# x1 = x + G p3: from two VectorE additions per pair to ScalarE copies and one accumulating DMA

## The chip, the cores and the metric

The kernel runs on 1 core of one Trainium2 chip. The metric is the device time of one execution in microseconds; three runs of the kernel before gave 2427.26, 2429.36 and 2429.52, so the median is 2429.36 us.

## The reference

Two layers work on x, 64 matrices of 256 x 256 in float32, with one adjacency matrix `adj` of 256 x 256.

```python
# --- layer 0 (adj_preln) ---
h = jnp.maximum(_layernorm(x, axis=-1), 0.0)
x = x + _L0_gnn_ref(h, adj, adj, L0_gnn_W1, L0_gnn_W2, L0_gnn_W3)
# --- layer 1 (adj_preln) ---
h = jnp.maximum(_layernorm(x, axis=-1), 0.0)
x = x + _L1_gnn_ref(h, adj, L1_gnn_W1, L1_gnn_b1, L1_gnn_W2, L1_gnn_b2)
```

Layer 0 multiplies three times by G = adj * adj and by a weight, with relu between: relu(G h W1), relu(G . W2), G . W3. Layer 1 needs U, the eigenvectors of the normalized Laplacian of adj (`jnp.linalg.eigh`), and computes U (relu(U^T h W1 + b1) W2 + b2). The sum that the change touches is the one that ends layer 0: x1 = x + G p3, with p3 = relu(...) W3.

## The kernel before

Two kinds of work share the core up to some 2250 us. The first is the eigenvector computation, class `Eigen`, called the chain here: tridiagonalization in 254 steps (`tridiagonalize`), then leaves, then four levels of merging. It is one long dependence, mostly small VectorE operations; a step also has two transposes on PE (`psB<-ident,ac` and `psA<-ident,A`, of a column that VectorE has just finished, `ac`), a square and a root on ScalarE and small operations on POOL (`m`, `q`, `qn`, `qs`, `gg`, `gu`, `none`, `xc`; in the second half of the steps only some of them).

The second is layer 0, class `Layers`, which doesn't need U. It runs over 32 pairs of matrices. It comes as two streams, that is, generators that yield one operation at a time:

- `products` yields for pair q: `third` (32 products of 512 columns, in the profile `bank<-y,L_gnn_W`), `turn_rows(q - 1)` (transposes, `bank<-eye,h`), half of `fourth` (256 columns, `bank<-L_gnn_W,s`), `for_layer1(q - 1)`, `first(q + 1)`, the other half of `fourth`, `second(q + 1)` and `last(q)` (four products of 512 columns, `bank<-p,gt`). Each group of products ends in a PSUM bank, of which there are four, and ScalarE empties it.
- `rows` yields the layer norms on ScalarE, with small VectorE operations between: `begin(q)` of x, and `norm1(q - 1)` of x1, whose result `turn_rows` transposes.

`last(q)` is the place of the change. Before, VectorE reads each of its two banks and adds x to it (`x<-x,bank`). Then SP writes x1 to DRAM ("spill"; not for the last two pairs), and `third(q + 1)` follows in the same generator.

The class `Pace` writes the order of all of this out by hand. It holds an estimated clock for each engine and, from the costs in `Op`, the time at which each tile is written or free (`busy` is how long an operation holds its engine, `until` when its result is there). For each operation of the chain, `chain` computes when it is due, and `run` first records operations of the streams that can start before that; of each stream only the operation at its head is seen (`Stream.head`). An operation that can't start before the limit stays at the head, and what is behind it in the generator stays unseen. PE and ScalarE keep the order that is so recorded (`manual_schedule`); VectorE, POOL and SP are ordered by the framework's scheduler. What is left of the streams when the chain has ended runs between the rounds of `layer1`, whose operations are all kept in the recorded order, and `pace.finish()` records the rest when round i = 8 begins (`LAST_AT - 1 - ahead`).

In the profile nearly all instructions have line 209, the line in `issue` that calls the recorded operation, or 213. They are told apart by their tiles.

Of the kernel before, what the change touches and what calls it, by code (L numbers as in the profile page):

```python
# [23 lines left out]
OP = mybir.AluOpType  # L24
# [58 lines left out]
class Op:  # L83
# [4 lines left out]
    def __init__(self, part, call, args, kwargs):  # L88
        self.part, self.engine, self.call, self.args, self.kwargs = part, ENGINES[part], call, args, kwargs
        self.name = call.__name__  # L90
        free = lambda a: int(np.prod([int(n) for n in a.shape[1:]]))
        named = dict(kwargs)
        outs = [named.pop("out")] if "out" in named else [args[0]]
        ins = [a for a in [*(args if "out" in kwargs else args[1:]), *named.values()] if isinstance(a, bass.AP)]
        total = named.pop("accum_out", None)
        if isinstance(total, bass.AP):
            outs.append(total)
            ins = [a for a in ins if a is not total]
        self.outs, self.ins = [span(a) for a in outs], [span(a) for a in ins]
        n = max(free(a) for a in outs[:1] + ins) if self.engine == "DVE" else free(outs[0])  # L100
        sums = len(outs) > 1

        if self.engine == "PE":
            self.columns = 0 if "transpose" in self.name else n
            self.busy = max(n * self.COLUMN, 0.224) if self.columns else 0.115
            self.until = max(self.busy, 0.165) + 0.35
        elif self.engine == "ACT":
            pointers = any(isinstance(kwargs.get(k), bass.AP) for k in ("scale", "bias"))
            self.busy = 0.13 + n / 1400 + 0.12 * pointers + 0.19 * sums
            self.until = self.busy + 0.12  # L110
        elif self.engine == "DVE":
            each = 6.3 if self.name == "reciprocal" else 2.0 if self.name == "tensor_tensor_scan" else 1.0
            pointers = self.name == "scalar_tensor_tensor" or any(a.shape[1:] == [1] for a in ins[1:])
            self.busy = 0.065 + 0.06 * pointers + each * n / 960 + 0.08 * sums
            self.until = self.busy + 0.125
        elif self.engine == "POOL":
            self.busy = 0.2 + 2 * n / 960
            self.until = self.busy + 0.1
        else:
            self.busy, self.until = 0.1, 4.0  # L120
# [13 lines left out]
def span(a):  # L134

    step = a.ap[0][0]
    lo = a.offset % step if step else a.offset
    return a.tensor.name, lo, lo + sum((int(n) - 1) * abs(int(s)) for s, n in a.ap[1:]) + 1
# [142 lines left out]
class Eigen:  # L281
# [998 lines left out]
    def level(self, n, qt, dc, rho, sg, bad=None):  # L1280
# [93 lines left out]
        def spread(ps, column):  # L1374

            for h in range(H):
                nc.tensor.matmul(
                    ps if last else ps[:, seg[h]],
                    lhsT=column[:, h : h + 1].to_broadcast([P, P]),
                    rhs=perm[:, h, :],  # L1380
                    start=h == 0 or not last,
                    stop=h == H - 1 or not last,
                )
# [349 lines left out]
class Layers:  # L1733
# [138 lines left out]
    def rows(self):  # L1872

        for q in range(PAIRS + 1):
            if q < PAIRS:
                if q > 0:
                    yield lambda: q - 1 in self.begun
                yield from self.begin(q)
            if q > 0:
                yield lambda: q - 1 in self.new  # L1880
                yield from self.norm1(q - 1)
# [101 lines left out]
    def last(self, q):  # L1983

        nc, x, p3 = self.nc, self.x.pop(q), self.p3.pop(q)
        x1 = self.kept.tile([P, H, 2, N], F32, tag="x1", name="x1")
        for m in range(H):
            ps = self.bank()
            yield from self.products_of(ps, [(self.gt2[:, h, m * P : (m + 1) * P], p3[:, h, :]) for h in range(H)])
            yield nc.vector.tensor_tensor(flat(x1)[:, m, :], flat(x)[:, m, :], ps, OP.add)  # L1990
        if q in self.spilled:
            yield nc.sync.dma_start(out=self.spilled[q], in_=x1.rearrange("p h b f -> p (h b f)"))
        else:
            self.x1[q] = x1
        self.new[q] = x1
# [111 lines left out]
    def layer1(self, pace):  # L2107


        ahead = 3  # L2110
        last = PAIRS - 1
        order = [*range(LAST_AT - 1), last - 1, last, *range(LAST_AT - 1, last - 1)]
        got = {i: self.fetch(order[i]) for i in range(ahead)}
        mid, tail = {}, {}
        with self.tc.manual_schedule():
            self.turn()
            pace.go_on(LOAD_US)
            for i in range(PAIRS + 2):
                if i == LAST_AT - 1 - ahead:
                    self.due = True  # L2120
                    pace.finish()
                if i + ahead < PAIRS:
                    got[i + ahead] = self.fetch(order[i + ahead])
                if i < PAIRS:
                    mid[i] = self.to_vectors(*got.pop(i))
                if 0 <= i - 1 < PAIRS:
                    s, xb = mid.pop(i - 1)
                    tail[i - 1] = self.from_vectors(s), xb
                if 0 <= i - 2:
                    self.finish(order[i - 2], *tail.pop(i - 2))  # L2130


def flat(t):
    return t.rearrange("p h b f -> p h (b f)")
# [63 lines left out]
```

## Time and profile before

| | us |
|---|---|
| median of three runs | 2429.36 |
| the profiled execution: first to last instruction | 2426.6 |
| PE idle in waits over 0.3 us, summed from the trace | 37.9 |
| tridiagonalization, from the first `ac` to the last | 21.9 to 1322 |
| VectorE's additions `x<-x,bank`, first and last start | 105.3 to 2249.8 |

The profiled execution's own time is its span; it lies 0.1% under the median and within 0.7 us of the fastest run. A row of the profile gives an engine, an operation, the written tile, an arrow and the read tiles, then how often, the busy time and the mean of one. In an order of time the first two columns are start and duration in us, and the brackets at the end give how long the engine stood idle before and what ended that. A float32 product appears as two records of PE, so that `x8` is four products. How full PE is over the span, in 40 equal slices, with the granted clock and the DMA engines below:

```profile
PE   7999999999999999999999899999999999999999
...
DVE  8999999999999999999999989999997888886443
ACT  4444454444444444344444244344344434443322
POOL 2334333343333111111111000000000000000443
PEclk9999999999999999999999999999999999999999
DMA  3000000000000000000000000000000000000676
```

DMAs before the change, with size and median time from issue to landing; all are issued by SP:

```profile
x<-x SPq DMA_DIRECT2D x60, 512.0 KB, 3.6
x<-in_x_dram SPq DMA_DIRECT2D x64, 256.0 KB, 3.7
```

The first row holds the spills of x1 and their loads back in layer 1.

### The profile page before, as it was taken

Reading aid. Unit: us, or ns where it says so; the run is one execution under the profiler, and the core shown is the slowest. Engines: PE = TensorE matmul, PEld = TensorE weight load, DVE = VectorE, ACT = ScalarE, POOL = GpSimd, SP = SyncE. Lnnn points to the kernel's source line nnn. Section 1 sums busy time; section 2 is a strip of 40 time slices with the busy share of each in tenths; the row PEclk is TensorE's granted clock in tenths of the full one; section 3 lists DMA queues with packets and bytes.
Section 4 is the critical chain, followed back from the end, with each engine's and each line's share of the span. In section 5 each row is a group of like instructions: output and inputs, shape, how many; then the busy total and the mean of one; then the engine's idle time right before and its main releaser. Section 6 shows DMA issues by size and latency. Waiting matters only on the chain. (4 is left out here: it accounts for less than half of the span.)

```text
span 2426.6 us, 38393 instructions
## 1 busy us (share of the span) xinstructions
PE 2381.5 (98%) x9226; PEld 1581.7 (65%) x9226; DVE 2127.2 (88%) x12971; ACT 1013.8 (42%) x2827; POOL 480.6 (20%) x1752
## 2 busy tenths in 40 slices
PE   7999999999999999999999899999999999999999
PEld 4666666666666566666666666666566666666788
DVE  8999999999999999999999989999997888886443
ACT  4444454444444444344444244344344434443322
POOL 2334333343333111111111000000000000000443
PEclk9999999999999999999999999999999999999999
DMA  3000000000000000000000000000000000000676
GB/s 113 18 21 7 23 23 18 23 23 23 6 23 23 18 22 23 22 6 23 23 23 26 10 23 23 23 23 22 18 22 27 22 23 12 16 22 1 210 255 204
DMA packets 59399, 90.02 MB, mean 37 GB/s; under 512 B 5792, under 2 KB 42784, under 8 KB 59168
## 3 DMA queue, kind: packets, MB, share of 16 engines
q1 hardware_dynamic: 59168, 87.52, 10.8%
q8 instruction: 74, 1.21, 0.2%
q14 instruction: 157, 1.29, 0.2%
HBM read 47.13 MB, written 40.37 MB: 36 GB/s over the span
## 5 line engine op out<-in xcount | busy, mean ns | idle before, releaser
L209 PE MATMUL bank<-y,L_gnn_W 128*128 128x512 f32 (+2 forms) x2182 | 903.5, 566 | 1.1 <-ACT y L209 1.1
L209 PEld LDWEIGHTS bank<-y,L_gnn_W 128*128 128x128 f32 x2182 | 401.8, 190 | 440.7 <-issue 419.0
L209 PE MATMUL bank<-L_gnn_W,s 128*128 128x256 f32 (+1 forms) x2092 | 465.2, 375 | 3.2 <-ACT s L209 3.2
L209 PEld LDWEIGHTS bank<-L_gnn_W,s 128*128 128x128 f32 x2092 | 386.7, 190 | 52.2 <-ACT s L209 3.9
L209 ACT ACTIVATE s<-bank 128x512 f32<-128x512 f32 x384 | 224.9, 586 | 196.4 <-PE bank L209 196.0
L209 PE MATMUL bank<-gt,s 128*128 128x256 f32 x1036 | 233.7, 379 | 2.8 <-ACT s L209 2.8
L209 PE MATMUL bank<-L_gnn_W,y 128*128 128x512 f32 (+2 forms) x542 | 230.9, 569 | 1.1 <-ACT y L209 1.1
L209 PEld LDWEIGHTS bank<-gt,s 128*128 128x128 f32 x1036 | 194.7, 191 | 39.7 <-issue 10.5
L209 ACT COPY y<-bank 128x512 f32<-128x512 f32 x192 | 111.5, 582 | 138.9 <-PE bank L209 138.6
L209 PEld LDWEIGHTS bank<-L_gnn_W,y 128*128 128x128 f32 x542 | 100.2, 190 | 97.3 <-issue 91.1
L209 POOL COPY m<-xr 128x1 f32<-128x1 f32 x254 | 55.8, 220 | 534.5 <-DVE xr L209 526.5
L209 ACT ACTIVATE s<-nn,guard 128x1 f32<-128x1 f32 x254 | 74.5, 293 | 208.1 <-DVE nn L209 169.0
L209 ACT ACTIVATE h<-x,shift,scale 128x256 f32<-128x256 f32 x256 | 137.3, 589 | 54.6 <-DVE shift L209 54.4
L209 ACT ACTIVATE junk<-x 128x256 f32<-128x256 f32 x256 | 105.6, 412 | 95.8 <-DVE x L209 80.5
L209 ACT ACTIVATE junk<-x,nm 128x256 f32<-128x256 f32 x256 | 129.0, 504 | 37.1 <-DVE nm L209 32.6
L209 DVE SCALAR_TENSOR_TENSOR A<-xr,wc,A 128x255 f32<-128x255 f32 (+63 forms) x381 | 139.9, 368 | 0.0
L209 DVE SCALAR_TENSOR_TENSOR A<-wr,q,A 128x255 f32<-128x255 f32 (+63 forms) x381 | 138.9, 366 | 0.0
L209 ACT ACTIVATE junk<-xr 128x254 f32<-128x254 f32 (+63 forms) x127 | 46.0, 362 | 216.5 <-DVE xr L209 211.4
L209 DVE SCALAR_TENSOR_TENSOR q<-q 128x1 f32<-128x1 f32 (+1 forms) x576 | 119.8, 208 | 13.0 <-ACT q L209 2.3
L209 PE MATMUL bank<-gt,h 128*128 128x256 f32 (+1 forms) x518 | 120.6, 382 | 0.1
L209 POOL TENSOR_TENSOR xb<-x,ub 128x512 f32<-128x512 f32 x16 | 19.9, 1271 | 495.5 <-DMA hw<-hw 485.6
L209 PE MATMUL bank<-p,gt 128*128 128x512 f32 (+2 forms) x270 | 117.0, 570 | 0.1
(615 smaller groups left out, 4306.2 us busy)
## 6 DMA issues: line engine op xcount, KB each, us to landing
x<-x SPq DMA_DIRECT2D x60, 512.0 KB, 3.6
x<-in_x_dram SPq DMA_DIRECT2D x64, 256.0 KB, 3.7
out_dram<-out SPq DMA_DIRECT2D x64, 256.0 KB, 2.2
hw<-hw SPq DMA_DIRECT2D x60, 256.0 KB, 2.7
L_gnn_W<-in_L_gnn_W_dram SPq DMA_DIRECT2D x1, 2048.0 KB, 10.9
L_gnn_W<-in_L_gnn_W_dram SPq DMA_DIRECT2D x1, 1024.0 KB, 13.5
L_gnn_W<-in_L_gnn_W_dram SPq DMA_DIRECT2D x1, 512.0 KB, 6.3
mask<-in_c_blk_dram SPq DMA_DIRECT2D x2, 256.0 KB, 3.1
```

What stands on the lines that cost most here:

```text
L209: return op.call(*op.args, **op.kwargs)
```

## The change

ScalarE now copies each of the two banks of `last` into x1, and one DMA per pair, issued by GpSimd (POOL), adds x to x1 in place; 64 additions on VectorE become 64 copies on ScalarE and 32 DMAs of 512 KB. The planner's costs get a line for such a DMA: it holds POOL for 1.1 us, and its result is there 5.0 us after its start.

```diff
@@ Op.__init__
             self.busy = 0.065 + 0.06 * pointers + each * n / 960 + 0.08 * sums
             self.until = self.busy + 0.125
+        elif self.engine == "POOL" and "dma" in self.name:
+            self.busy, self.until = 1.1, 5.0
         elif self.engine == "POOL":
             self.busy = 0.2 + 2 * n / 960
             self.until = self.busy + 0.1
@@ Layers.last
         for m in range(H):
             ps = self.bank()
             yield from self.products_of(ps, [(self.gt2[:, h, m * P : (m + 1) * P], p3[:, h, :]) for h in range(H)])
-            yield nc.vector.tensor_tensor(flat(x1)[:, m, :], flat(x)[:, m, :], ps, OP.add)
+            yield nc.scalar.copy(flat(x1)[:, m, :], ps)
+        rows = lambda t: t.rearrange("p h b f -> p (h b f)")
+        yield nc.gpsimd.dma_start(out=rows(x1), in_=rows(x), accum_op=OP.add)
         if q in self.spilled:
             yield nc.sync.dma_start(out=self.spilled[q], in_=x1.rearrange("p h b f -> p (h b f)"))
         else:
```

## The prediction

> **What bounds the kernel now.** I read the busy shares first, then the matrix engine's waits.
>
> ```profile
> PE 2381.5 (98%) x9226; PEld 1581.7 (65%) x9226; DVE 2127.2 (88%) x12971; ACT 1013.8 (42%) x2827; POOL 480.6 (20%) x1752
> ...
> L209 DVE TENSOR_TENSOR x<-x,bank x64: 624/680/689, 105.3 to 2249.8; 128x512 f32<-128x512 f32 x64
> ...
> PE bank L209 <- ACT s L209: 6.5, 7, 2.4
> PE psC L209 <- DVE c L209: 6.3, 1, 6.3
> ...
> PE psB L209 <- DVE xr L209: 3.9, 8, 1.0
> ...
> PE psB L209 <- DVE ac L209: 3.2, 6, 1.1
> ```
>
> PE is busy for 2381.5 of 2426.6 us, and its waits of over 0.3 us sum to 38. The end is therefore set by how full the planner keeps PE's queue: the time that an engine beside it saves is worth nothing in itself, and every hole in the order of PE's products is lost. Where holes can come from shows in PE's order of time around one `last` (four 512-wide products are eight records here).
>
> ```profile
> 946.23 0.27 PE L209 MATMUL psB<-ident,ac 128*128 128x128 f32 x1
> ...
> 950.56 0.27 PE L209 MATMUL psB<-ident,ac 128*128 128x128 f32 x1
> ...
> 951.21 3.60 PE L209 MATMUL bank<-p,gt 128*128 128x512 f32 x8
> 955.44 0.29 PE L209 MATMUL psB<-ident,ac 128*128 128x128 f32 x1 [0.62 <-DVE xr L209]
> 955.57 0.27 PE L209 MATMUL psA<-ident,A 128*128 128x128 f32 x1
> 955.68 1.88 PE L209 MATMUL bank<-y,L_gnn_W 128*128 128x512 f32 x4
> ```
>
> Between two pairs of the chain's transposes (`psB<-ident,ac`) lies one step of the tridiagonalization, filled with products of layer 0. After `last` (`p,gt`) the next pair's `third` (`y,L_gnn_W`) follows at once. The chain has hardly a margin: its own part of a step shows on VectorE.
>
> ```profile
> 953.70 0.68 DVE L209 TENSOR_TENSOR x<-x,bank 128x512 f32<-128x512 f32 x1
> ...
> 955.07 0.22 DVE L209 SCALAR_TENSOR_TENSOR ac<-A,m,xa 128x1 f32<-128x1 f32 x1
> ```
>
> From the transpose at 950.56 the chain needs until 955.29 to have the next `ac`, plus 0.15 to PE's start: 4.88 us, of which the add is 0.68, so 4.20 without it. Products for less than that in a step leave PE idle.
>
> **The change part by part.**
>
> *The adds go.* 64 x 0.68 = 43.4 us leave VectorE. They bind PE only where PE waited for a step with an add: waits such as the 0.62 above, 5.6 us over the tridiagonalization. This is the only direct gain.
>
> *Copies come.* 64 copies of 128x512 at 582 ns (row `y<-bank`, 111.5 us for 192) are 37 us on ScalarE, 42% busy. They empty a bank in 0.58 us in place of 0.68, and four banks cover some 14 us of products: nothing. Were ScalarE full, it would be 37.
>
> *The hole behind every DMA (the main term).* `products` is one generator, and the planner sees one operation of it at a time. Behind `last`'s copies it now gives the DMA, then the spill on SP, then the products of the next `third`. The planner's new branch has the DMA's result ready 5.0 us after its start, so the spill can't start sooner, and `run` records it only when the chain's next due time lies beyond. Until then the chain's transposes go into PE's queue with no products between them. Before, an add stood there, 0.72 us in the planner's costs (0.065 + 512/960 + 0.125). The built program's order shows it: 18 of the first 253 steps hold under 3.1 us of products (at 14 of the 18 pairs; six hold only the two transposes), where neighbours hold 3.5 to 6. A 512-wide product costs 0.86 us: five between 1104.05 and 1108.34 in PE's order of time. A 256-wide costs 0.43: seven between 1086.16 and 1089.18. So priced, the 18 steps hold 23.9 us in all. The chain's part of these steps, worked out as above at each and taken as the median of nine neighbours, is 6.2 us at the first and 3.5 to 3.7 at the last, 81.3 in sum. PE idles 81.3 - 23.9 = 57.4. From the other side: when the tridiagonalization ends (1322 us now), the new order has 76.7 us less of products behind it. The chain can be shorter by its 36 adds at most, 24.5; so the loss is at least 52.2, and 76.7 if it gets no shorter. Four pairs have no such step, but fall short by less; I let that stand against the 5.6 gained and take **57**, ends 52 and 76.7. After the tridiagonalization the deficit grows by only 15 us up to the flag, as much as the adds of 12 pairs (16): no further loss there.
>
> *The clock behind a hole.* The granted clock fell twice in this execution.
>
> ```profile
> 1344.74 1.19 PE L209 MATMUL psD<-bs,mask 128*128 128x128 f32 x4 [2.77 <-DVE rb L209]
> ...
> 1343.00:1346.00 3.00, 1.26 (x5) 1.29 (x6) 3.00 (x26) 0.69 (x2) 0.00 (x0) 0.74 0.00 0
> 1346.00:1350.00 4.00, 3.56 (x16) 2.84 (x15) 2.60 (x18) 0.96 (x2) 0.00 (x0) 0.77 0.17 66
> ...
> 1715.56 4.97 PE L209 MATMUL bank<-gt,s 128*128 128x256 f32 x14 [2.40 <-ACT s L209]
> ```
>
> The column behind POOL's is the granted clock: 3 x 0.26 + 4 x 0.23 = 1.7 us lost behind a gap of 2.77, and after the gap of 2.40 seven products took 4.81 in place of 3.02. A gap of 1.57 at 2251 cost nothing (clock 1.00). The new holes are 2.3 to 5.1 us long at 14 places; I charge 13 of them 1.7: **22**, ends 0 (the fall lies wholly in the gap) and 44. [...]
>
> *The end of layer 0 (second term).* `layer1` ends the streams at its eighth round. Before, pair 31's `last` ended at 2249.75 and its `turn_rows` began at 2289.10, with layer 1's products between. The new order, 92 us of products behind at the flag, has `turn_rows` of pair 31 directly behind its `last`. PE then waits for copy, DMA and norm. The norm lasts from 2199.09 to 2206.68 at pair 30 with two evictions in it, 6.5 without. The DMA isn't in this trace. Below stands the spill of the same 512 KB, 3.6 us to landing; above the load of 2048 KB, 10.9. I take 5.5, near the spill: a second operand is another 512 KB, 1.6 us at the 334 GB/s of q1 (87.52 MB in 10.8% of 2426.6), and 0.3 for the issue. 0.8 + 5.5 + 6.5 less 1.2 that the first transposes gain: **12**, ends 10 and 17, and 1.7 for the clock. [...]
>
> *What queues behind.* On POOL the DMA's issue stands between the chain's small operations; POOL waits 1.07 to 3.0 us for VectorE before `gg` and `m`, and 17 of the 18 DMAs of this stage stand ahead of such a wait. An issue costs between SP's 0.34 and 1.27 (POOL's longest operation, `xb`). On ScalarE `norm1`'s first reading waits for the landing, and the chain's square and root behind it. It was placed for 5.0 us; a landing d later costs about d x d / (2 x 5.1) for each of 18 pairs (step 5.1 us, next chain operation at a random place): nothing at 5.5, 61 us at 10.9. The chain has no margin, so I take **4** for both, ends 0 and 84. On SP the next x load waits behind the spill for some 5 us more; its norm ends 7 us or more before its first product in every pair now, and `norm1` 9.9 before `turn_rows`: covered, and some 2 us a pair for seven pairs if the DMA took 10.
>
> Sum: 57 + 22 + 13.7 + 4 = 97. The profiled execution, 2426.6 of span, is taken to stand for the median, 2429.4 (0.1% away). **2526 us.**
>
> **Rivals.** (1) *A slow DMA*: it lands after 8 to 11 us and ScalarE's queue carries the wait into the chain. For: two operands, and an issue from an engine that is 30% busy in this stage (391.66 of 1305 us). Against: the same bytes land in 3.6. At 10.9: 61 + 5 more, 2592. (2) *Short holes only*: the clock costs nothing and the holes 52, the end 10: 2491; a little under it if some holes are filled. For: the fall of the clock comes some 2.4 us after the gap's start and lasts 3.4, so part of it lies inside the longer holes. (3) *Not slower*: VectorE's chain, not PE, sets the end; rid of 43.4 us it ends sooner and pulls the rest along, 2386. For: VectorE is 88% busy and the chain has no margin. Against: PE idles for only 38 us in all. It decides only if the products missing in the holes run elsewhere in time that was idle, which is less than the 57 needed. (4) *Nothing*: the holes are of the plan alone and don't show. The trace has PE's instructions in the program's order throughout, so I see no way.
>
> **How the numbers follow.** The forecast (2491 to 2555) has 0.72, the slow DMA 0.14, under 2491 but slower 0.10, (3) 0.02, (4) 0.02. The range 2485 to 2575 leaves out half of the slow DMA and most of the smaller loss. A change within 0.2% (5 us) can't be told from none here. Faster 0.02, same 0.02, slower 0.96.
>
> **What would show it.** Right: PE waits for `psB<-ident,ac` of 2.3 to 5 us once per pair up to about 1310 us, new and some 60 us in sum; a granted clock of 0.7 to 0.8 behind them; one wait of about 12 us before the last `eye,h`; PE's busy time up by the clock alone. Wrong: `junk<-x` on ScalarE waiting for a DMA by more than 1 us in most pairs (rival 1), POOL's `qs` or `gg` late, or PE's waits as short as now.

## The result, and the profile after

The changed kernel takes 2524.16 us (median of 4 runs, 2523.11 to 2524.55); the kernel before, run beside it, 2429.44 (4 runs). The ratio is 1.0392, 95% interval 1.0378 to 1.0405: 95 us slower. The profiled execution has a span of 2521.3 us, against 2426.6.

The page of the changed kernel: busy shares, PE over the span, POOL's issues of the new DMAs, and the DMA's median time to landing.

```profile
PE 2409.3 (96%) x9198; PEld 1589.8 (63%) x9198; DVE 2088.6 (83%) x12907; ACT 1049.9 (42%) x2891; POOL 509.5 (20%) x1784
...
PE   7999999999999999999999999999999999999799
...
L211 POOL DMA_DIRECT2D x<-x x32 | 28.6, 895 | 546.9 <-ACT x L211 463.1
...
x<-x POOLq DMA_DIRECT2D x32, 512.0 KB, 4.6
```

VectorE lost 38.5 us of work (2127.2 to 2088.6), ScalarE gained 36.1, and neither shows in the time. PE decides: it is busy 27.8 us longer (2409.3 against 2381.5) though it computes the same products, and it is idle for 112.0 us (2521.3 - 2409.3) where it was idle for 45.1. 27.8 + 66.9 is the whole difference of the spans, 94.7. So there are two things to find: the idle time, and why the same products take longer.

The idle time, from PE's waits in the changed kernel (total us, times, longest):

```profile
PE psB L211 <- DVE xr L211: 57.5, 29, 5.0
PE bank L211 <- ACT h L211: 15.6, 5, 12.6
...
PE psB L211 <- DVE ac L211: 4.6, 1, 4.6
```

The first row was 3.9 us in 8 before. The second has one wait of 12.6 us at the end of layer 0. One of the waits for `xr`, behind the first `last`, in order of time (start, duration; the brackets hold the idle time before and what ended it):

```profile
105.10 0.38 PE L211 MATMUL psB<-ident,ac 128*128 128x128 f32 x2
...
105.54 0.81 PE L211 MATMUL bank<-p,gt 128*128 128x384 f32 x2
...
107.29 1.07 POOL L211 DMA_DIRECT2D x<-x  x1 [1.74 <-ACT x L211]
...
111.38 0.40 PE L211 MATMUL psB<-ident,ac 128*128 128x128 f32 x2 [5.03 <-DVE xr L211]
...
111.97 1.06 PE L211 MATMUL bank<-y,L_gnn_W 128*128 128x512 f32 x1
112.03 0.34 SPq L211 DMA_DIRECT2D x<-x  x1
```

The step from 105.10 to 111.38 holds 0.81 us of products. The next pair's `third` (`y,L_gnn_W`) comes only behind the next transpose, at 111.97. None of its products reads what the DMA writes; they simply stand behind it in PE's order. The engine that "released" PE, VectorE, was on its ordinary chain.

The same products take longer because of the clock. In the windows of the changed kernel around that hole (PE busy is the second number, the granted clock stands before the last two):

```profile
109.00:112.00 3.00, 0.62 (x5) 0.65 (x6) 2.73 (x17) 0.05 (x1) 1.62 (x7) 0.95 0.86 162
112.00:115.00 3.00, 3.00 (x5) 1.30 (x5) 2.95 (x13) 1.26 (x6) 0.78 (x3) 0.50 0.70 226
115.00:118.00 3.00, 3.00 (x8) 1.31 (x7) 2.90 (x16) 2.13 (x9) 1.61 (x6) 0.98 0.35 123
```

PE is "busy" throughout 112 to 115, but at half clock (0.50). The records of 512 columns start every 0.85 us from 111.97 to 114.53 and every 0.43 us from 115.25 on: in 3.4 us behind the hole PE gets done what takes 1.7 at the later pace.

### The profile page after: what moved, and what is told of

It reads as the page before. It is cut to its first block, busy times and chain, and to the rows that moved or that the text cites. A ratio compares the mean times of both kernels' runs of the same rounds, so it can differ in the third digit from the quotient of the medians.

```text
span 2521.3 us, 38400 instructions
## 1 busy us (share of the span) xinstructions
PE 2409.3 (96%) x9198; PEld 1589.8 (63%) x9198; DVE 2088.6 (83%) x12907; ACT 1049.9 (42%) x2891; POOL 509.5 (20%) x1784
## 3 DMA queue, kind: packets, MB, share of 16 engines
HBM read 47.13 MB, written 40.37 MB: 35 GB/s over the span
## 5 line engine op out<-in xcount | busy, mean ns | idle before, releaser
L211 PE MATMUL bank<-y,L_gnn_W 128*128 128x512 f32 (+3 forms) x2160 | 928.8, 581 | 1.3 <-ACT y L211 1.1
L211 PEld LDWEIGHTS bank<-y,L_gnn_W 128*128 128x128 f32 x2160 | 407.4, 195 | 440.0 <-issue 415.4
L211 PE MATMUL bank<-L_gnn_W,s 128*128 128x256 f32 x2092 | 469.3, 376 | 4.4 <-ACT s L211 4.4
L211 PE MATMUL bank<-gt,s 128*128 128x256 f32 (+1 forms) x1038 | 233.0, 377 | 0.4 <-ACT s L211 0.4
L211 ACT COPY y<-bank 128x512 f32<-128x512 f32 x192 | 111.5, 583 | 145.7 <-PE bank L211 145.3
L211 ACT ACTIVATE h<-x,shift,scale 128x256 f32<-128x256 f32 x256 | 137.8, 591 | 64.4 <-DVE shift L211 64.1
L211 PE MATMUL psB<-ident,ac 128*128 128x128 f32 x381 | 86.7, 282 | 62.6 <-DVE xr L211 57.5
L211 POOL DMA_DIRECT2D x<-x x32 | 28.6, 895 | 546.9 <-ACT x L211 463.1
L211 PEld LDWEIGHTS psB<-ident,ac 128*128 128x128 f32 x381 | 47.4, 137 | 128.7 <-issue 99.3
```

The lines of the kernel that those rows point to most:

```text
L211: return op.call(*op.args, **op.kwargs)
```

## The experiments

The theory was that the loss lies in the planner's order: the spill, which needs the DMA's result, stands at the head of the serial generator `products`, and 5.0 us of planned time pass with no products for PE. Its rivals were the DMA itself, ScalarE's wait for its landing, and the end of layer 0 alone.

**The planned delay without the DMA.** Kernel before (VectorE's adds, no copies, no DMA on POOL), the second add of a pair merely planned as late as the DMA:

```diff
-            yield nc.vector.tensor_tensor(flat(x1)[:, m, :], flat(x)[:, m, :], ps, OP.add)
+            op = nc.vector.tensor_tensor(flat(x1)[:, m, :], flat(x)[:, m, :], ps, OP.add)
+            if m == H - 1:
+                op.until = 5.72
+            yield op
```

> The kernel before (additions on VectorE, no copy, no DMA on POOL), with one number of the plan changed: the second addition's result is taken to be there 5.72 us after its start. Theory: the order has 16 short steps and 65 us less of products behind the tridiagonalization than before, and the additions still lengthen the chain: 2429 + 65 + some 20 for the clock = 2514, between 2490 and 2530, without any part of the change. Rivals 1 and 3 (DMA, ScalarE, POOL): 2429.

Measured: 2529.43 us, ratio 1.0415 (1.0399 to 1.0431). Its waits of PE:

```profile
PE psB L209 <- DVE xr L209: 64.1, 30, 5.7
...
PE bank L209 <- ACT h L209: 6.5, 3, 5.5
...
PE psB L209 <- DVE ac L209: 5.7, 3, 2.6
```

A number in the planner alone, with every operation of the old kernel kept, costs 100 us. It is 15 us above the theory's number. PE's waits in the tridiagonalization rose by 61.7 us, near the 65 expected; but PE's busy time rose by 30.7 us (2412.2 against 2381.5), where some 20 were charged for the clock, and the waits behind the tridiagonalization rose by 11.3, 5.5 of them at the end of layer 0, for which nothing was charged. Next to the changed kernel the holes are longer, 64.1 and 5.7 us in place of 57.5 and 4.6. That the adds, which still lie in the chain here, are the reason was not tried.

**DMA and spill moved out of the products.** Both are yielded at the head of `norm1`, in the stream of the norms, where what follows needs them anyway:

```diff
@@ Layers.last
-        rows = lambda t: t.rearrange("p h b f -> p (h b f)")
-        yield nc.gpsimd.dma_start(out=rows(x1), in_=rows(x), accum_op=OP.add)
-        if q in self.spilled:
-            yield nc.sync.dma_start(out=self.spilled[q], in_=x1.rearrange("p h b f -> p (h b f)"))
-        else:
+        if q not in self.spilled:
             self.x1[q] = x1
-        self.new[q] = x1
+        self.new[q] = x1, x
@@ Layers.norm1
-        x1 = self.new[q]
+        x1, x = self.new[q]
+        rows = lambda t: t.rearrange("p h b f -> p (h b f)")
+        yield self.nc.gpsimd.dma_start(out=rows(x1), in_=rows(x), accum_op=OP.add)
+        if q in self.spilled:
+            yield self.nc.sync.dma_start(out=self.spilled[q], in_=rows(x1))
```

> The changed kernel, with the accumulating DMA and the spill yielded by the stream of the norms (at the head of norm1) in place of the stream of products; same instructions. Theory (holes in PE's order behind each DMA): the built order has 2 steps under 3.1 us instead of 18, and 24 us of products between the last pair's products and its transposes. PE's waits for psB fall from some 60 us to under 10, the clock stays at 0.99 or more, no wait of 12 us at the end: 2420 to 2435 us. Rival 1 (ScalarE and POOL, waiting for the DMA, hold up the chain): nothing they wait for has changed, 2500 or more. Rival 2 (only the end's wait): 2505 to 2512.

Measured: 2424.22 us, ratio 0.9984 (0.9974 to 0.9993). The whole loss is gone, with the copies, the 32 DMAs and their landing times kept.

The same with layer 1's rounds able to run on to the twentieth (`LAST_AT = 20`):

> As the run before it in this list, with the last two pairs put at place 20 of layer 1's order instead of 12, so 65 us of products stand between the last pair's products and its transposes. Theory: the end's wait was covered already by 24 us, so within 4 us of that run; the 5.6 us of PE's waits at steps with an addition are gone for good, so 2418 to 2428, at or a little under the kernel before. Rival 1: 2500 or more.

Measured: 2424.68 us, ratio 0.9987 (0.9978 to 0.9996). Without the deficit of products there is no wait at the end to win back.

**Only the spill moved.** The DMA stays behind `last`'s copies, the spill alone goes to the head of `norm1`:

```diff
@@ Layers.last
         yield nc.gpsimd.dma_start(out=rows(x1), in_=rows(x), accum_op=OP.add)
-        if q in self.spilled:
-            yield nc.sync.dma_start(out=self.spilled[q], in_=x1.rearrange("p h b f -> p (h b f)"))
-        else:
+        if q not in self.spilled:
             self.x1[q] = x1
@@ Layers.norm1
         x1 = self.new[q]
+        if q in self.spilled:
+            yield self.nc.sync.dma_start(out=self.spilled[q], in_=x1.rearrange("p h b f -> p (h b f)"))
```

> The changed kernel with the accumulating DMA left behind `last`, and only the spill on SP moved to the head of `norm1`, so that nothing behind the DMA in the serial generator of products waits for its result. Theory (what costs is the spill's wait at the head of that generator): no short step, 2420 to 2430 us, as with both moved. [...]

Measured: 2424.32 us, ratio 0.9979 (0.9969 to 0.9989). The same place in PE's order of time, in this kernel:

```profile
105.21 0.38 PE L211 MATMUL psB<-ident,ac 128*128 128x128 f32 x2
...
105.64 0.81 PE L211 MATMUL bank<-p,gt 128*128 128x384 f32 x2
106.29 5.31 PE L211 MATMUL bank<-y,L_gnn_W 128*128 128x512 f32 x12
111.48 0.41 PE L211 MATMUL psB<-ident,ac 128*128 128x128 f32 x2
```

`third` follows `last` at once and the transpose waits for nothing. So it isn't the DMA's place or its issue on POOL that costs, but one instruction on an otherwise idle queue, the spill, that has products of another pair behind it in the generator's order.

**The end of layer 0 alone.** The changed kernel with `LAST_AT = 20` in place of 12, nothing else:

> The changed kernel with layer 1's rounds able to go on to the twentieth before the streams are ended: 34 us of layer 1's products now stand between the last `last` and the last `turn_rows`, the 18 short steps of the tridiagonalization are untouched. Theory (the end of layer 0 is a term of its own, 12.6 us of wait and up to 1.7 of clock): 2509 to 2512 us, a PE wait for `h` of under 1 us there, psB waits as before (some 57 us). Rival (the end's wait is a part of the loss by the short steps, and moves elsewhere): 2522 to 2526.

Measured: 2507.12 us, ratio 1.0315 (1.0298 to 1.0332). Its waits of PE:

```profile
PE psB L211 <- DVE xr L211: 57.5, 29, 5.0
...
PE bank L211 <- ACT h L211: 2.6, 3, 1.7
```

The holes of the tridiagonalization are untouched, the end's wait is gone, and 17.0 us with it (13.1 by the spans of the two profiled executions). The end is a term of its own.

**Holes filled with work that nobody needs.** The changed kernel with 53 products more in 14 pairs, whose results nobody reads:

```diff
+        fill = {0: 5, 2: 5, 5: 5, 6: 2, 7: 4, 8: 2, 9: 4, 10: 2, 11: 4, 12: 5, 13: 3, 14: 4, 15: 4, 16: 4}.get(q, 0)
+        if fill:
+            ps = self.bank()
+            yield from self.products_of(ps, [(self.gt2[:, h % H, 0:P], p3[:, h % H, :]) for h in range(fill)])
         rows = lambda t: t.rearrange("p h b f -> p (h b f)")
```

> The changed kernel with 53 products of 128x512 more behind `last` in 14 of the pairs, whose results nobody reads: 45.6 us of PE's time (53 x 0.86) put into the short steps. Theory (the holes cost PE its clock besides the idle time): the holes are filled, the fall of the clock goes with them, and the time falls by 15 to 22 us although PE has 46 us more to do: 2502 to 2510, PE busy some 2430, psB waits under 20 us. Rival 1 (the idle time is the whole cost, the clock none): 2521 to 2526. Rival 2 (the products missing there are not what PE waits for): 2565 to 2572.

Measured: 2501.89 us, ratio 1.0294 (1.0277 to 1.0311): 22.3 us faster with 45.6 us more to compute. The page and, in a fence of its own, the known place in PE's order of time:

```profile
PE 2432.3 (97%) x9320; PEld 1601.7 (64%) x9320; DVE 2087.6 (83%) x12907; ACT 1047.1 (42%) x2891; POOL 508.8 (20%) x1784
```

```profile
105.60 5.10 PE L211 MATMUL bank<-p,gt 128*128 128x384 f32 x12
111.44 0.40 PE L211 MATMUL psB<-ident,ac 128*128 128x128 f32 x2 [0.74 <-DVE xr L211]
```

The 5.03 us of waiting are now 0.74. PE's waits in the tridiagonalization fall from 60.4 to 16.3 us, 44 us, as much as the useless work. That exchange is worth nothing; what is left over is the clock. PE's busy time less the 45.6 us is 2386.7, 22.6 under the changed kernel's. The clock's own records say the same: in the tridiagonalization of the changed kernel it fell 12 times and stood at half for 51.2 us, in 44.6 of which PE was busy, so 22.3 us of work were lost; here it doesn't fall there at all (mean clock of the execution 0.995, against 0.984). The experiment separates the two terms without touching the useful work: 22 us for the clock behind these holes.

**ScalarE's wait, first with the spill left in place.** The changed kernel with the planner's time to the DMA's result set to an add's:

```diff
-            self.busy, self.until = 1.1, 5.0
+            self.busy, self.until = 1.1, 0.72
```

> The changed kernel with one number of the plan changed: the DMA's result is taken to be there after 0.72 us, an addition's figure, instead of 5.0. The instructions are the same, their order differs. Theory: 4 short steps instead of 18, so the holes go (57 us and their clock, 22), but the norm's first reading now stands too early in ScalarE's queue, by some 4 us, and the chain's square and root wait behind it: 4 x 4 / (2 x 5.1) = 1.6 us for each of 18 pairs, 28 us: about 2455, between 2435 and 2480. Rival 1 (the waits for the DMA are the loss): earlier readings make it worse, over 2524. Rival 3 (the DMA itself, whatever the order): 2524.

Measured: 2491.38 us, ratio 1.0266 (1.025 to 1.0282). The direction was right, the size not: 33 us came back where some 70 were expected. Four short steps were left, and ScalarE waited 152 us for landings in 32 waits. To part the two, the same number in the kernel with only the spill moved, which has no short step:

> As the kernel with only the spill moved, but the planner takes the DMA's result as ready after 0.72 us in place of 5.0: no short steps, and the norm's readings stand on ScalarE some 4 us ahead of the landing. It measures the wait on ScalarE alone. Theory (that wait made up most of what was left in the kernel with 0.72 us and the spill in place: 62 us over the kernel before): 2470 to 2495 us, ScalarE's `junk` waiting for the DMA some 150 us in 32 waits. Rival (what was left there was the spill's place and four short steps, the wait on ScalarE costs by d x d / (2 x 5.1), some 28 us at 4 us): 2450 to 2460 or less.

Measured: 2501.03 us, ratio 1.0293 (1.0276 to 1.031), somewhat above the theory's span and far above the rival's. It is 76.7 us above the same kernel with 5.0. ScalarE's waits for the landing and, in a fence of its own, one of them in order of time:

```profile
ACT junk L211 <- DMA x<-x: 145.7, 32, 7.3
```

```profile
470.17 0.29 ACT L211 ACTIVATE s<-nn,guard 128x1 f32<-128x1 f32 x1
...
471.13 0.91 POOL L211 DMA_DIRECT2D x<-x  x1
...
474.99 0.40 DVE L211 SCALAR_TENSOR_TENSOR xr<-xr,f,r 128x182 f32<-128x182 f32 x1
...
475.74 0.42 ACT L211 ACTIVATE junk<-x 128x256 f32<-128x256 f32 x1 [5.28 <-DMA x<-x]
...
479.39 0.34 ACT L211 ACTIVATE junk<-xr 128x181 f32<-128x181 f32 x1
479.63 0.19 ACT L211 ACTIVATION_READ_ACCUMULATOR junk<-xr 128x1 f32 x1
479.86 0.22 DVE L211 SCALAR_TENSOR_TENSOR nn<-xr,m 128x1 f32<-128x1 f32 x1 [0.49 <-ACT junk L211]
...
481.39 0.41 PE L211 MATMUL psB<-ident,ac 128*128 128x128 f32 x2 [2.69 <-DVE ac L211]
```

The DMA starts at 471.13, and ScalarE stands idle for 5.28 us until it has landed and the norm's first reading (`junk<-x`) can start. What the chain's square (`junk<-xr`) reads is written by 475.39, but the square stands behind several of the norm's readings in ScalarE's order and runs only at 479.39; VectorE waits for it, and PE for VectorE. The planner had placed the reading for a result 0.72 us after the DMA's start. A number too small in a plan costs nearly as much as a number that leaves holes in the order.

**The other way: 6.5 us.** The kernel with only the spill moved, and 6.5 in place of 5.0:

> As the kernel with only the spill moved, with 6.5 us in place of 5.0 as the planner's time to the DMA's result, so that the norm's readings are placed behind the landing. Theory (what that kernel still has of waits of ScalarE for the landing, 42 us in 27, is nearly free): 2420 to 2427 us, within 0.2% of it, the waits under 20 us. Rival (these short waits still hold up the chain): 2412 to 2419.

Measured: 2425.60 us, ratio 0.9987 (0.9978 to 0.9996). ScalarE's waits for the landing in this kernel:

```profile
ACT junk L211 <- DMA x<-x: 8.5, 8, 2.0
```

They fell from 42.4 us in 27 to 8.5 in 8, and the time didn't move. Short waits of ScalarE are free here; 5.0 was a sound number. The four kernels rid of the holes lie within 1.4 us of each other, 0.13% to 0.21% faster than the kernel before.

## Why the prediction was right

The forecast was 2526 us, 2524.16 were measured. Its steps:

*The holes: 57 forecast, 54.8 measured* (60.4 us of waits over 0.3 us in the tridiagonalization, less the 5.6 that were there before). Counting the products between two transposes in the built order, and taking them from the chain's own part of a step, gave the idle time to 4%. The second way of reckoning, 76.7 us less of products behind the tridiagonalization, was read too narrowly. The last `ac` now starts at 1323.2 in place of 1322.3, so the stage lost 76.7 + 0.9 = 77.6 us. That is not a bound for the holes: it is holes and clock together, 54.8 + 22.8. The prediction's 57 and 22 sum to 79.

*The clock: 22 forecast, 22.3 to 22.6 measured* by filling the holes, 22.3 by the clock's records. This rules out the rival "short holes only", whose point was that the fall lies inside the gap: of the 51.2 us at half clock only 6.6 lie in idle time, worth 3.3. That the size fits so closely is in part luck. The prediction charged 13 holes with one fall of 3.4 us each; it was 12 falls, three of them twice as long, less the part inside the gaps. PE's whole busy time is 27.8 us up; the rest is the end's clock (3.8 us) and scattered falls.

*The end of layer 0: 13.7 forecast; undoing it alone gave 17.0 by the medians, 13.1 by the spans.* The terms were mis-sized against each other. The end in the changed kernel's order of time:

```profile
2367.19 0.59 ACT L211 COPY x<-bank 128x512 f32<-128x512 f32 x1 [1.13 <-PE bank L211]
2368.07 0.88 POOL L211 DMA_DIRECT2D x<-x  x1 [48.53 <-ACT x L211]
...
2372.71 0.42 ACT L211 ACTIVATE junk<-x 128x256 f32<-128x256 f32 x1 [4.94 <-DMA x<-x]
...
2379.06 2.07 ACT L211 ACTIVATE h<-x,shift,scale 128x256 f32<-128x256 f32 x4 [1.05 <-DVE shift L211]
...
2379.72 0.48 PE L211 MATMUL bank<-eye,h 128*128 128x128 f32 x1 [12.57 <-ACT h L211]
```

From 2367.15, where PE stopped, to 2379.72: 0.92 for the copy and the hand-over, 4.6 for the DMA, 7.0 for the norm up to its first quarter. The DMA was taken 0.9 too long, the norm up to there 1.7 too short (6.5 less 1.2). The clock was taken at 1.7 and stayed at half for 17.07 us, of which 8.7 lie behind the wait; by PE's busy time in them that cost 3.8 us. In this trace the whole term is thus 11.3 us more of idle time and 3.8 of clock, 15.1.

*The DMA: 5.5 us forecast, 4.6 measured* (issue on POOL 0.9, between the ends 0.34 and 1.27). The forecast started from a row that it misread: 3.6 us is the median of 30 spills and 30 loads back together. The spills alone stand in the changed kernel's first 2230 us, beside the DMAs of the same size on POOL:

```profile
x<-x POOLq DMA_DIRECT2D x30, 512.0 KB, 4.6
x<-x SPq DMA_DIRECT2D x30, 512.0 KB, 3.0
```

They landed in 3.0 us before, too. With that in the prediction's sum the DMA would have come to 4.9. It took 1.6 more than a spill; how much of that is the accumulation, the issue on POOL or the other destination was not tried.

*POOL and ScalarE: 4 forecast, about nothing.* Of the 66.9 us of new idle time 54.8 lie in the holes and 11.3 at the end (14.3 against 3.0 us of waits behind 2230 us); 0.8 are left. The kernel with only the spill moved keeps the DMA on POOL and 42.4 us of waits on ScalarE, and is no slower.

*The slow DMA, rival 1,* didn't come about; its mechanism did when the plan was given 0.72 us, and there its price was wrong. In the kernel with only the spill moved and 0.72, by d x d / (2 x 5.1) the 17 waits of the tridiagonalization (72.8 us) should cost 32.2; PE's waits in that stage rose by 35.1 (40.7 less 5.6). So the formula holds for the idle time. Left out were the pairs behind it (12.3 us more of waits) and the clock (PE busy 24.4 us longer). 35.1 + 12.3 + 24.4 = 71.8, and the time rose by 71.8 over the kernel before (72.5 by the spans of the profiled executions). In the prediction, 2592 for this rival lacked its clock too.

*"Not slower", rival 3,* is refuted by the kernels without holes: with VectorE rid of the adds and PE kept full, the last `ac` comes 15.5 us earlier (1306.8 with only the spill moved), but PE has done some 18 us less by then, as its waits up to there are no shorter (8.2 against 5.6 us), and 4.9 us of 43 come out at the end. PE's work is the bound, as the prediction had it.

## What to carry to other kernels

In an order that is worked out before the kernel runs, an instruction that waits is a wall for everything its generator yields after it, even when it stands on a queue that is itself idle: put a late consumer into the stream of those who need its result, not ahead of work that doesn't. Price a planned delay by the work that is missing at the engine that sets the time, read from the built order, and add the clock that the hole costs behind it (22 us here beside 54.8 of idle time); and set the planner's duration no shorter than the landing that is measured (here 4.6 us, where 5.0 and 6.5 did equally well), since behind too small a number the engine that waits holds up what its recorded order puts next: with 0.72 ScalarE waited 145.7 us for landings, and the time rose by 77 us.

## What the runs showed of the hardware

*When the clock fell.* In the changed kernel, its first 30 us left out, the clock's records show half clock 16 times within the span: 12 times for 3.41 us, three times for 6.83, once for 17.07 (at the end of layer 0). PE waited 18 times for 2.0 us or more; with 16 of these waits the clock fell, 1.2 to 5.4 us after the wait's start, and with two it didn't (2.35 us up to 861.10 and 3.19 up to 1236.67). Two waits of the changed kernel, and the windows behind them (the clock before the last two numbers):

```profile
555.01 0.40 PE L211 MATMUL psB<-ident,ac 128*128 128x128 f32 x2 [2.11 <-DVE xr L211]
...
1236.67 0.29 PE L211 MATMUL psB<-ident,ac 128*128 128x128 f32 x1 [3.19 <-DVE xr L211]
```

```profile
555.00:558.00 3.00, 2.99 (x7) 1.50 (x8) 2.87 (x16) 0.43 (x2) 1.01 (x5) 0.57 0.92 175
...
1238.00:1242.00 4.00, 4.00 (x12) 1.82 (x11) 3.93 (x37) 2.85 (x11) 0.72 (x4) 1.00 0.65 207
```

The clock fell to half at 555.43, behind the wait of 2.11 us; with that of 3.19 it stayed at 1.00 from 1233 to 1242. So the length of a wait alone doesn't tell in this trace whether the clock falls; what does was not shown.

*The accumulating DMA beside a busy VectorE.* 512 KB, added to x1 in place, landed in 4.6 us (median of 32) with VectorE busy for 83% of the span; the traffic with HBM was the same before and after (47.13 MB read, 40.37 written). An issue held POOL for 0.86 to 1.07 us.
